# A two-layer graph kernel: narrow gathers straight into their place, the rank-9 term as nine rows of a list, three joints overlapped

## The chip, the cores and the metric

The kernel runs on one core of a Trainium2 chip. The metric is the device time of one execution in microseconds (us). Engines: PE (TensorE, matrix products), PEld (its weight loads), DVE (VectorE), ACT (ScalarE), POOL (GpSimd), SP (SyncE, which here only issues DMAs). DMAs are issued by SP, by ACT and, where the rows to be fetched stand in a list of indices, by POOL ("gathers", `DMA_INDIRECT` in the profile).

## The reference, cut to what matters

`x` is 8 x 2048 x 128 (batch, node, feature), `adj` is a 2048 x 2048 matrix, nearly all zeros, whose nonzero pattern is symmetric; the weights and the 640 x 128 `Theta1` are dense. All is float32.

```
sj = x @ w_j ; si = x @ w_i
res = si[:, :, None] + sj[:, None, :] + adj * w_r + g_b       # 8 x 2048 x 2048
x = layernorm(x + einsum('bij,bjd->bid', res, x) @ weight + bias0)
# twice the same support: A1 = A2 = adj
h1 = einsum('bnf,nw->bwf', x, adj) ; h2 = 2 * einsum('bnf,nw->bwf', h1, adj) - x
x = layernorm(x + relu(concat(x, h1, h2, h1, h2) @ Theta1 + bias))
```

The first layer splits into `adj * w_r` times Y0 = x @ weight, and a term of rank 9: the eight columns si (one for each batch) times column sums of Y0, and one row that is the same for all nodes. The second layer is done by Horner's rule: u = X1 th0, y = adj^T u + X1 th1, out = adj^T y + X1 th2, where X1 is the result of layer 0. So the matrix is applied three times: in layer 0, in "hop 1" (from u to y) and in "hop 2" (from y to out).

## The kernel before, in words

Nodes are cut into 16 chunks of 128. A row of Y0, u or y (8 batches x 128 features) is 4 KB, and a chunk of rows fills one of the slots of 128 x 1024 numbers in the tiles `Y` (16 slots), `ring` (6), `trp` (1, `spare`) and `st` (4).

Stage A (up to some 150 us): the 16 row blocks of adj are loaded (`pump`, lines 216 to 232), transposed on PE and scaled by w_r on ACT (`row_groups`). The transposed blocks go into DRAM tensors `rr_d`, beside a plain copy of the matching columns of adj. x is loaded, transposed and multiplied by the weight (`x_t`, `y_of`), and Y0 goes to DRAM (`y0_d`). Masks of nonzero 32-wide tiles are made on DVE.

Lists (120 to 193 us): DVE sorts the nonzero rows of each chunk's columns into seven lists of up to 128 row numbers: four "T" lists (each serves 32 columns of the chunk), two "H" lists (64 columns each) and a third H list (all 128 columns). A chunk of a product is then: the diagonal block (`own_rows`, line 765), four T products and three H products (`listed`, line 722), each with 128 gathered 4-KB rows as moving operand and gathered pieces of adj as weights. T lists hold only rows of chunks 0 to 13, so they can be fetched before the last two chunks are written.

The weights are gathered as well, by jobs (lines 524 to 581). For chunks 4 to 15, `get_job` gathers rows of 1 KB from `rr_d` into one of four staging slots of `st`, three or four gathers to a job, and `keep_job` masks them on DVE into `rct` (for layer 0) and `rc` (for the hops); 24 jobs, 84 gathers. Chunks 0 to 3 need pieces of adj for the hops alone: eight more jobs, 28 gathers of 512-byte rows into `trp[:, 2]`, masked by DVE into `rc`. The source text puts them last: they are kept in hop 1 (line 924).

Chunks 0 to 3 of layer 0 are multiplied in full (`full_rows`, 16 blocks each). Chunks 4 to 15 go by lists in a loop (lines 839 to 862): own rows, rank-9 term (`si_t`, a transpose of si, and `rank9`, two products with 5 rows), T, H, sum with x (`z_add`), layernorm, then `make_u` for the chunk two steps before (transposes to `x1t`, product with th0, store into `u_d`). x for the sum is loaded by `load_z` into one of four slots, and the own rows of Y0 by `own0`: chunks 4 to 7 still stand in `Y`, chunks 8 to 15 are read back from DRAM.

Gathered rows of Y0, u and y go round twelve slots of `Y` (`G`, line 710), whose slots come free when the product that reads them is done. Hops (`hop`, line 865): own rows, theta product, T and H of each chunk, begun one ahead. At the start of hop 1, two chunks are begun with their T lists while the last chunk's u is on its way.

All engines' instructions are recorded in order of the text, and a scheduler then places them; an instruction of POOL that is ready may go ahead of one that the text has earlier. The order on each queue is fixed when the program is built.

Of the kernel before, what the change touches and what calls it, by code (L numbers as in the profile page):

```python
# [18 lines left out]
def kernel(  # L19
# [36 lines left out]
    PAD = 40000  # L56
    W = 3 * P
# [57 lines left out]
    def load_constants():  # L115
        with nc.allow_non_contiguous_dma(reason="two columns of 128 numbers"):
            act.dma_start(out=wx[:, D:D + 2], in_=g_w[0:2 * D].rearrange("(t p) -> p t", p=P))
        act.dma_start(out=wx[:, 0:D], in_=weight)
        act.dma_start(out=wr, in_=g_w[2 * D:2 * D + 1][None, :].to_broadcast([P, 1]))
        act.dma_start(out=gb, in_=g_b[None, :].to_broadcast([P, 1]))  # L120
        for i in range(4):
            act.dma_start(out=b0row[:, i, :], in_=bias0[None, :])
        act.dma_start(out=b1bc[:, 0, :], in_=bias1[None, :].to_broadcast([P, D]))
        act.dma_start(out=th, in_=theta.rearrange("(m p) f -> p m f", p=P))

    ctx.enter_context(nc.allow_non_contiguous_dma(reason="512-byte rows of a block of 128 columns"))
    load_constants()
# [4 lines left out]
    e5 = const.tile([1, 5], F32)  # L132
    dve.memset(e5, 0.0)
    dve.memset(e5[:, 4:5], 1.0)
# [4 lines left out]
    sel5 = const.tile([P, 4, 5], F32)  # L139
    dve.memset(sel5, 0.0)  # L140
    for i in range(4):
        dve.tensor_copy(sel5[:, i, i:i + 1], sel[:, 0:1])
        dve.tensor_copy(sel5[:, i, 4:5], sel[:, 1 + i:2 + i])
# [3 lines left out]
    dve.tensor_copy(num, numi)  # L147
    coli = const.tile([P, NI], I32)
    pool.iota(coli[:, 0:NT], pattern=[[1, NC], [0, QT]], base=0, channel_multiplier=0)
    pool.iota(coli[:, NT:NT + 2 * NC], pattern=[[1, NC], [0, 2]], base=0, channel_multiplier=0)  # L150
# [12 lines left out]
    si = const.tile([P, NC, 37], F32)  # L163
    dve.memset(si, 0.0)
    for h in range(2):
        dve.memset(si[:, :, 32 * h + 4:32 * h + 5], 1.0)
# [34 lines left out]
    todo += [("x", 8), ("s", 12), ("x", 9), ("s", 13), ("x", 10), ("x", 11), ("s", 14), ("x", 12)]  # L201
# [11 lines left out]
    def load_z(c):  # L213
        zs[c] = load_x(c, [ring[:, 3], ring[:, 4], ring[:, 5], spare][(c - 2) % 4])

    def pump():
        while todo:
            what, n = todo[0]
            if what == "a" and n < done["a"] + 3:
                sp.dma_start(out=am[n % 3], in_=adj[R_ORDER[n] * P:(R_ORDER[n] + 1) * P, :])  # L220
            elif what == "x" and n < done["x"] + 6:
                c = X_ORDER[n]
                xin[c] = load_x(c, ring[:, X_SLOT[n % 6]])
                if c < ND:
                    zs[c] = xin[c]
            elif what == "s" and done["a"] == NC:
                store_rt(n)
            elif what == "c" and done["a"] == NC:
                copies([n])
            else:  # L230
                return
# [53 lines left out]
    def s_rows(c0):  # L285
# [5 lines left out]
        for h in range(2):  # L291
            act.copy(si[:, c4, 32 * h:32 * h + 4], sraw[:, c4, h * HB:(h + 1) * HB, 1])
# [15 lines left out]
    LAST = list(range(ND)) + list(range(8, NC)) + list(range(4, 8))  # L308
# [18 lines left out]
    pump()  # L327
    for k, n in enumerate(R_ORDER):
# [139 lines left out]
    def lists_end(part):  # L468
# [17 lines left out]
        s = slice(lo, hi)  # L486
        rown = small.tile([P, NT], F32, name=f"rown{part}", tag="rown")[:, 0:hi - lo]
# [4 lines left out]
        dve.scalar_tensor_tensor(rown, rown, float(NC), col[:, s], op0=ALU.mult, op1=ALU.add)  # L492
# [14 lines left out]
    adj128 = adj.rearrange("n (c f) -> (n c) f", f=P)  # L507
# [17 lines left out]
    for c in range(ND):  # L525
        jobs += [("T", c), ("H", c)]
    got, kept = [0], [0]
    last = trp[:, 2].rearrange("p i f -> p (i f)")

    def staged(k):  # L530
        return st[:, k % 4 * BD:] if jobs[k][1] >= ND else last

    def get_job():
# [3 lines left out]
        for n, i in enumerate(columns(c, what)):  # L537
            if c >= ND:
                gather(
                    s[:, n * 2 * P:(n + 1) * 2 * P], rr_d[c - ND].rearrange("n m f -> n (m f)"), idx,  # L540
                    i, N,
                )
            else:
                gather(s[:, n * P:(n + 1) * P], adj128, idr, i, N * NC)

    def keep_job():
# [3 lines left out]
        m = 2 if c >= ND else 1  # L550
        hc = has[:, columns(c, what)[0]:columns(c, what)[0] + QT]
        for k in range(m):
            if m == 1 or k == 1:
                to = rc[:, c * W:(c + 1) * W]
            else:
                to = rct[:, (c - ND) * W:(c - ND + 1) * W]
            of = s[:, k * P:]
            if what == "T":
                if m == 2:
                    dve.tensor_mul(  # L560
                        to[:, 0:P].rearrange("p (t f) -> p t f", t=QT),
                        strided(of, QT, m * P + TW, TW), hc[:, :, None].to_broadcast([P, QT, TW]),
                    )
                    continue
                for t in range(QT):
                    at = t * (P + TW)
                    dve.tensor_scalar(
                        to[:, TW * t:TW * t + TW], of[:, at:at + TW], hc[:, t:t + 1], None,
                        op0=ALU.mult,
                    )  # L570
                continue
            step = m * P + 64
            dve.tensor_mul(
                to[:, P:2 * P].rearrange("p (t f) -> p t f", t=2), strided(of, 2, step, 64),
                hc[:, 0:2, None].to_broadcast([P, 2, 64]),
            )
            i = NT + 2 * NC + c
            dve.tensor_scalar(
                to[:, 2 * P:3 * P], of[:, 2 * m * P:2 * m * P + P], has[:, i:i + 1], None,
                op0=ALU.mult,  # L580
            )

    def make_ub():
# [4 lines left out]
        for h in range(2):  # L588
            pe.matmul(
                pu[32 * h:32 * h + 5], e5, b0row.rearrange("p i f -> p (i f)"), start=True,  # L590
# [444 lines left out]
```

## Time and profile before

| what | value |
|---|---|
| time, median of 3 runs (lowest, highest) | 855.64 us (852.42, 857.48) |
| the profiled execution's own time | 818.08 us |
| its span, first to last instruction | 816.3 us |
| PE busy, POOL busy, DVE busy | 732.8, 445.2, 394.7 us |
| mean granted PE clock | 0.971 |
| moved by DMA | 253.90 MB, mean 311 GB/s |
| share of the 16 DMA engines' time: POOL's queue, SP's, ACT's | 49.7%, 31.1%, 8.9% |

The profiled execution is 4.4% faster than the median of the timed ones. Stages by the trace: adj and x up to 151 us, lists and full rows up to 262 us, layer 0 by lists up to 429 us, joint and hop 1 up to 625 us, hop 2 up to 801 us, and a tail up to 816 us.

How to read it: the page cuts the span into 40 slices of 20.4 us and gives the busy tenths of each engine in each; "DMA" is the mean busy share of the 16 DMA engines. A group row names engine, operation, output and input, count, busy time and mean length of one, and what the engine waited for before it. A POOL gather is busy for the time that POOL takes to issue it; the data land later. All lines of this kernel are recorded by one helper (L72), so that operations are told apart by the tiles they touch.

### The profile page before, as it was taken

The page shows a single profiled execution, that of the slowest core. Times are in us where ns is not written, and L with a number is a line of the kernel's source. Part 1 is how long each engine was busy: PE and PEld are TensorE (multiplying, and loading weights), DVE is VectorE, ACT ScalarE, POOL GpSimd, SP SyncE. Part 2 cuts the span into 40 slices and gives each one's busy share as a digit, 9 for nine tenths or more (in the row PEclk, how much of TensorE's full clock was granted, in tenths as well). Part 3 has the DMA queues.
Part 4 walks back from the last instruction along what each step waited for, and adds up shares of the span by engine and source line. Part 5 has one row for each costly group of instructions (what it writes and reads, how often), then busy time and mean ns, then how long its engine had stood idle before and what let it go on. Part 6 is the DMA issues. An engine that isn't in the chain of part 4 may idle for free.

```text
span 816.3 us, 10067 instructions
## 1 busy us (share of the span) xinstructions
PE 732.8 (90%) x3554; PEld 364.9 (45%) x3554; DVE 394.7 (48%) x591; ACT 192.7 (24%) x439; POOL 445.2 (55%) x432
## 2 busy tenths in 40 slices
PE   4999999997999998988798888898899999999992
PEld 4666566642644343434345243333344454444441
DVE  4664876578341655555533000000100377777775
ACT  3757554321200332313222000000000011111101
POOL 1000000477747876776344677776774777776740
PEclk9999999997999999999899899999999999999997
DMA  8999999999326799999969799899999799999982
GB/s 264 296 314 316 352 292 295 314 398 347 119 89 223 244 346 368 341 344 367 356 224 344 246 364 360 314 365 346 339 372 357 252 343 357 370 385 389 363 299 68
DMA packets 165299, 253.90 MB, mean 311 GB/s; under 512 B 17255, under 2 KB 118020, under 8 KB 163192
## 3 DMA queue, kind: packets, MB, share of 16 engines
q0 software_dynamic: 49280, 146.52, 49.7%
q1 hardware_dynamic: 93200, 81.01, 31.1%
q10 hardware_dynamic: 22760, 25.63, 8.9%
q8 instruction: 30, 0.49, 0.2%
q14 instruction: 29, 0.24, 0.1%
HBM read 234.82 MB, written 58.72 MB: 360 GB/s over the span
## 4 chain that ended last, share of the span: by engine, by line
PE 52%; DMA 29%; issue 6%; ACT 6%; DVE 3%; POOL 2%; ACTq 0%; POOLq 0%; SPq 0%; DVEq 0%
PE bank L72 52%; DMA Y<-u_d,idx 12%; DMA Y<-y_d,idx 8%; DMA st<-rr_d,idx 2%; DMA rd<-rr_d 2%; ACT Y L72 2%; DMA ring<-in_x_dram 2%; POOL Y L72 1%; ACT rct L72 1%; ACT trp L72 1%; DMA trp<-in_adj_dram,idr 1%; DVE s L72 1%; DVE ring L72 1%; ACT at L72 1%; DVE st L72 1%
## 5 line engine op out<-in xcount | busy, mean ns | idle before, releaser
L72 POOL DMA_INDIRECT Y<-y_d,idx x196 | 212.0, 1081 | 93.2 <-PE bank L72 38.0
L72 PE MATMUL bank<-Y,rc 128*32 128x512 f32 (+2 forms) x896 | 219.7, 618 | 21.3 <-DMA Y<-u_d,idx 19.1
L72 POOL DMA_INDIRECT st<-rr_d,idx x84 | 90.3, 1075 | 183.5 <-DVE rown L72 148.3
L72 POOL DMA_INDIRECT Y<-u_d,idx x112 | 111.8, 999 | 53.9 <-issue 29.9
L72 PEld LDWEIGHTS bank<-Y,rc 128*32 128x32 f32 (+2 forms) x896 | 58.6, 130 | 179.3 <-issue 99.5
L72 PE MATMUL bank<-Y,at 128*128 128x512 f32 x256 | 115.2, 601 | 0.0
L72 PE MATMUL bank<-Y,rct 128*32 128x512 f32 (+2 forms) x336 | 77.3, 625 | 8.5 <-DMA Y<-y_d,idx 8.5
L72 DVE TENSOR_REDUCE s<-sq 128x4 f32<-128x512 f32 x64 | 43.9, 686 | 58.0 <-ACT sq L72 58.0
L72 PEld LDWEIGHTS bank<-Y,at 128*128 128x128 f32 x256 | 47.8, 193 | 53.6 <-issue 53.4
L72 DVE COPY ring<-bank 128x512 f32<-128x512 f32 x10 | 6.9, 692 | 110.1 <-PE bank L72 110.1
L72 ACT ACTIVATE sq<-ring 128x512 f32<-128x512 f32 x44 | 27.7, 630 | 129.5 <-DVE ring L72 109.7
L72 PE MATMUL bank<-ring,rd 128*128 128x512 f32 x108 | 51.5, 599 | 5.7 <-DMA rd<-rr_d 4.1
L72 PE MATMUL bank<-ident,rc 128*128 128x128 f32 (+2 forms) x302 | 45.0, 297 | 12.6 <-DMA rc<-in_adj_dram 6.6
L72 PE MATMUL bank<-th,at 128*128 128x128 f32 x384 | 49.2, 283 | 1.9 <-ACT at L72 1.9
L72 PEld LDWEIGHTS bank<-th,at 128*128 128x128 f32 x384 | 46.8, 197 | 6.7 <-ACT at L72 3.8
L72 DVE TENSOR_TENSOR ring<-bank,ring 128x512 f32<-128x512 f32 x26 | 17.3, 688 | 66.0 <-PE bank L72 60.8
L72 DVE TENSOR_REDUCE st<-rc 128x64 f32<-128x2048 f32 x16 | 36.5, 2283 | 25.7 <-DMA rc<-in_adj_dram 25.7
L72 ACT COPY ring<-bank 128x512 f32<-128x512 f32 x34 | 19.9, 586 | 122.5 <-PE bank L72 112.9
L72 PEld LDWEIGHTS bank<-Y,rct 128*32 128x32 f32 (+2 forms) x336 | 20.8, 130 | 57.3 <-issue 32.4
L72 PEld LDWEIGHTS bank<-ident,rc 128*128 128x128 f32 (+2 forms) x302 | 33.8, 150 | 25.5 <-issue 9.1
L72 PE MATMUL bank<-wx,trp 128*128 128x130 f32 x256 | 36.9, 288 | 4.3 <-ACT trp L72 2.2
L72 PE MATMUL bank<-ident,ring 128*128 128x128 f32 x232 | 32.5, 282 | 6.4 <-DMA ring<-in_x_dram 2.8
(142 smaller groups left out, 789.1 us busy)
## 6 DMA issues: line engine op xcount, KB each, us to landing
rc<-in_adj_dram SPq DMA_DIRECT2D x16, 1024.0 KB, 10.9
ring<-in_x_dram SPq DMA_DIRECT2D x25, 512.0 KB, 8.5
rr_d<-in_adj_dram SPq DMA_DIRECT2D x12, 1024.0 KB, 10.8
rr_d<-Y SPq DMA_DIRECT2D x8, 1024.0 KB, 9.0
y_d<-Y SPq DMA_DIRECT2D x16, 512.0 KB, 10.6
u_d<-ring ACTq DMA_DIRECT2D x12, 512.0 KB, 7.0
ring<-y_d SPq DMA_DIRECT2D x11, 512.0 KB, 23.2
ring<-u_d SPq DMA_DIRECT2D x10, 512.0 KB, 3.9
```

The costliest lines, as they stand in the source:

```text
L72: return lambda *a, **k: tc.keep_in_program_order(f(*a, **k))
```

## The change

Seven things change together.

1. Start: each load of adj is cut into two halves; w_r is the first constant to be loaded, on ACT's queue, and the constants of later stages go to SP's queue, after the first eight chunks of x.
2. Pieces of adj for chunks 0 to 3: no staging and no mask by DVE. `rc[0:1536]` is zeroed by POOL, and 28 gathers write rows of 32, 64 or 128 numbers (128, 256 or 512 bytes) straight into their places; an index out of bounds leaves the zeros.
3. Jobs of the other chunks: the same 84 gathers, more of them placed before the loop of layer 0 and fewer in it.
4. Rank 9, chunks 4 to 15: the third H list is held to 119 entries, and its last nine rows carry si (in the weights, by `si_rows`) and the rows of `ub` (in two slots `C0`, by `ub_rows`). `rank9` and `si_t` stay for chunks 0 to 3 only. In this input the third lists have 73 to 112 entries.
5. x of chunks 4 to 15 is loaded into `x1t[c]`, where the transposed result is written later. Own rows of Y0 stay in place for chunks 4 to 11.
6. Slots: layer 0 gathers into ten slots (`G0`: eight of `Y`, two of `ring`) and two for the third list (`C0`); the hops use twelve of `Y` (`G1`).
7. Joints: two blocks of `full_rows(2)` go ahead of the end of the lists; hop 1 begins three chunks, not two; the last two chunks of hop 2 are done by halves of the batch (`by_halves`).

As built, POOL's queue has 58 gathers before its first gather of Y0 for a chunk's T list in the kernel before (54 of jobs, 4 of chunk 0), and 92 and the memset in the changed one (60 of jobs, all 28 direct ones, and 4 of Y0 for the third lists of chunks 4 and 5 and two T lists of chunk 5 that go ahead). The seventh and last gather for chunk 4 is the 101st, that for chunk 15 the 196th. In hop 1 no gather of adj is left (20 before).

```diff
+    LC = 96
+    R9 = 23
...
     def load_constants():
+        act.dma_start(out=wr, in_=g_w[2 * D:2 * D + 1][None, :].to_broadcast([P, 1]))
...
             if what == "a" and n < done["a"] + 3:
-                sp.dma_start(out=am[n % 3], in_=adj[R_ORDER[n] * P:(R_ORDER[n] + 1) * P, :])
+                for w in (slice(0, N // 2), slice(N // 2, N)):
+                    sp.dma_start(
+                        out=am[n % 3][:, w], in_=adj[R_ORDER[n] * P:(R_ORDER[n] + 1) * P, w]
+                    )
...
     acc0, acc1 = acc_pair(), acc_pair()
     pump()
+    load_constants()
...
     def load_z(c):
-        zs[c] = load_x(c, [ring[:, 3], ring[:, 4], ring[:, 5], spare][(c - 2) % 4])
+        zs[c] = load_x(c, x1t[c])
...
-    LAST = list(range(ND)) + list(range(8, NC)) + list(range(4, 8))
+    LAST = list(range(ND)) + list(range(12, NC)) + list(range(4, 12))
...
+        if part:
+            dve.tensor_scalar(pl[:, 2 * NC:], pl[:, 2 * NC:], free, None, op0=ALU.mult)
...
     jobs = [("T", c) for c in T_ORDER] + [("H", c) for c in range(ND, NC)]
-    for c in range(ND):
-        jobs += [("T", c), ("H", c)]
...
+    def get_direct(n):
+        for at, w, i in direct[:n]:
+            gather(
+                rc[:, at:at + w], adj.rearrange("n (c f) -> (n c) f", f=w), idr, i, N * (N // w)
+            )
+        del direct[:n]
...
+    def si_rows(c0):
+        b = by4(bank[turns[turn[0] % len(turns)]])[LC:]
+        turn[0] += 1
+        for i in range(4):
+            pe.matmul(
+                b[:, i, :], si[:, c0 + i, :], ident, start=True, stop=True, skip_group_check=True,
+                tile_position=(0, LC),
+            )
+        r = rct.rearrange("p (c w) -> p c w", w=W)
+        act.copy(r[LC:, c0 - ND:c0 - ND + 4, 2 * P:3 * P], b)
...
-    NG = 12
-    G = [flat(Y[:, n]) for n in LAST[:NG]]
+    G0 = [flat(Y[:, n]) for n in LAST[:8]] + [flat(ring[:, n]) for n in range(2)]
+    C0 = [flat(ring[:, 5]), flat(spare)]
+    G1 = [flat(Y[:, n]) for n in list(range(4)) + list(range(8, NC))]
...
     def own0(c):
-        load_own(0, y0_d, c, Y[:, c] if c < 8 else ring[:, c % 2], c < 8)
+        load_own(0, y0_d, c, Y[:, c] if c < 12 else ring[:, 3 + c % 2], c < 12)
...
     rank9(1, acc1)
+    ub_rows(C0)
+    for c in range(ND, NC, 4):
+        si_rows(c)
     rounds2([5, 6])
     next_job()
     rounds2([7])
+    acc2 = bank[4:6]
+    full_rows(2, acc2, LAST[:2])
     lists_end(1)
     z_add(acc0, zs[0])
     z_add(acc1, zs[1])
+    pool.memset(rc[:, 0:ND * W], 0.0)
...
     rank9(2, acc2)
+    next_job()
+    next_job()
     z_add(acc2, zs[2])
...
-        if c < 15:
+        if kept[0] < len(jobs):
             keep_job()
-        if c < 13 or c == 14:
+        if c % 2 == 0 and got[0] < len(jobs):
             get_job()
+        get_direct(1 if c < 10 else 2 if c < 12 else 3)
         accs = acc_pair()
         own_rows(0, c, accs, True)
         if c + 2 < NC:
             own0(c + 2)
-        rank9(c, accs)
-        if c + 1 < NC:
-            si_t(c + 1)
         listed(0, c, accs, "T")
         listed(0, c, accs, "H")
...
         begin(0)
+        if i == 1:
+            fetch(2)
+            rows(2, "T")
         between()
         begin(1)
+        if i == 1:
+            begin(2, bank[4:6])
...
         for k, c in enumerate(order):
+            if i == 2 and k >= NC - 2:
+                rows(k, "H")
+                rows(k + 1 if k + 1 < NC else NC, "T")
+                by_halves(k)
+                continue
```

In `by_halves`, for each half of the batch, PE does the transposes of X1 first, then the theta, own, T and H products of that half, and DVE and ACT work on a half (add, relu, mean, square, then scale and store 256 KB) while PE does the next.

## The prediction

> **What bounds the kernel now.** I read the page's slices first, then the busy time by stretch, then POOL's and PE's instructions in order of time.
>
> Slices of the page: PE, POOL, DMA.
>
> ```profile
> PE   4999999997999998988798888898899999999992
> POOL 1000000477747876776344677776774777776740
> DMA  8999999999326799999969799899999799999982
> ```
>
> PE, POOL and DMA are all near full from slice 15 to slice 38, so no total names the bound; slices 11 to 13 (204 to 265 us) are the only long hole of the DMA engines. Stretches of the span (us, busy time and count of PE, PEld, DVE, ACT, POOL, then PE clock, DMA share, GB/s): layer 0 by lists, joint, hop 1 with and without gathers of adj, hop 2, tail.
>
> ```profile
> 240.00:430.00 190.00, 172.01 (x792) 76.81 (x791) 95.59 (x168) 48.26 (x99) 126.23 (x122) 0.98 0.89 309
> 430.00:476.00 46.00, 37.74 (x188) 17.75 (x187) 7.41 (x12) 7.46 (x14) 26.95 (x27) 0.93 0.87 303
> 476.00:580.00 104.00, 95.03 (x430) 38.49 (x428) 8.82 (x25) 5.01 (x9) 76.38 (x78) 0.97 0.96 351
> 580.00:625.00 45.00, 42.04 (x197) 18.02 (x197) 3.26 (x6) 2.84 (x5) 32.69 (x34) 0.96 0.98 365
> 640.00:801.00 161.00, 160.95 (x821) 77.28 (x818) 121.00 (x166) 23.41 (x45) 112.80 (x99) 1.00 0.96 344
> 801.00:816.00 15.00, 0.35 (x4) 0.11 (x2) 7.40 (x10) 1.56 (x3) 0.00 (x0) 0.67 0.25 74
> ```
>
> Hop 2 is bound by PE (160.95 of 161), the tail by a DVE chain. For the rest, POOL in order of time:
>
> ```profile
> 223.66 1.00 POOL L72 DMA_INDIRECT st<-rr_d,idx  x1 [0.30 <-issue]
> 224.96 0.99 POOL L72 DMA_INDIRECT st<-rr_d,idx  x1 [0.30 <-issue]
> 234.74 1.00 POOL L72 DMA_INDIRECT st<-rr_d,idx  x1 [8.79 <-DVE rc L72]
> ...
> 239.55 1.00 POOL L72 DMA_INDIRECT Y<-y_d,idx  x1 [0.31 <-issue]
> ...
> 554.83 1.00 POOL L72 DMA_INDIRECT trp<-in_adj_dram,idr  x1 [0.30 <-issue]
> ```
>
> A gather costs POOL 1.0 us and 0.3 us until the next, 1.30 us whatever its width: 128 KB for `st` or 440 KB for `Y`. From 476 to 580 us it issues 78 in 104 us, hardly pausing: its queue, not the products, sets hop 1. PE's theta products, one row where a chunk begins, show it:
>
> ```profile
> 571.78 1.95 PE L72 MATMUL bank<-th,at 128*128 128x128 f32 x16
> 581.88 1.95 PE L72 MATMUL bank<-th,at 128*128 128x128 f32 x16
> 596.49 1.95 PE L72 MATMUL bank<-th,at 128*128 128x128 f32 x16
> 605.63 1.95 PE L72 MATMUL bank<-th,rct 128*128 128x128 f32 x16
> 614.77 1.95 PE L72 MATMUL bank<-th,rct 128*128 128x128 f32 x16
> ```
>
> A chunk after gathers of adj takes 14.6 us (581.88 to 596.49), without them 9.14 us, which is PE's own work.
>
> **What the Trainium skill says.** "DMA: Bandwidth & Descriptors", Issuing engines are not separate DMA queues: all issuers share 16 DMA engines. The trace agrees: the queues' shares add to 89.7% of the span, so bytes from any queue compete. The same page, Specifications: below 512 B a transfer loses line rate; the page counts 17,255 packets under 512 B but not whose, so no run here shows what the change's 128-byte rows cost. "TensorE: Matmul & The Clock Gate", its table of properties: GpSimd's queue is strict FIFO; the 8.79 us wait above held 2 more adj gathers and then the first Y0 gather, which agrees. The same page, Part 1: The HAM clock gate: an idle window of about 3.4 us halves PE's clock; after a wait of 4.58 us at 451.66 us the H products of two chunks took 11.68 us, 5.84 each, against 3.85 for a chunk's at full clock, which agrees.
>
> **Step 1, start: -3 us.** PE first has x at 16.48 us, after idling 1.22, 0.68 and 2.79 us; SP waited 4.9 us for a constant's DMA before it could issue x at 6.54. Halves let PE begin earlier, and x no longer waits for that constant. From then on PE and ACT take turns at 12.4 us per two blocks without a DMA wait. Gain between 0 (DMA share is 1.02 from 20 to 151 us, so earlier demand may find no data) and 4.7 us (the three idles); I take 3. The moved constants (0.4 MB, about 1.2 us of DMA) lie where x is prefetched.
>
> **Step 2, POOL ahead of chunk 4: +19 us.** The first job is issued at 151.7, now 148.7. 92 gathers x 1.30 us, the memset (1.4 us, as `st`'s 128x1536 took) and about 1 us of waits for `st` slots put the first T gather of chunk 4 at 271, against 239.55. Its last is number 101: 148.7 + 2.4 + 100 x 1.30 = 281; landing 6.5 us (median of `st` gathers; `Y` 8.4 in a full queue), last products 2 us: chunk 4 ends at 290. Before, it ended at 270.8. The 8.79 us wait goes, as two jobs are kept ahead of `z_add(acc2)`. An added wait: DVE now keeps five H jobs (chunks 4 to 8) ahead of chunk 3's sum, the last gathered near 280 and landed near 286; behind it stand chunk 3's sum and layernorm and chunk 4's sum, and PE, which needs chunk 3's banks for chunk 5. That falls near 290, so it is hidden; uncovered it would cost the few us by which 286 passes the need. x for chunk 4 and on waits for what was in `x1t` (loads of `Y` rows, pieces of `rct`); behind it on SP's queue stand diagonal blocks and own rows, a chunk ahead of their use. PE, done with full rows at 262, will idle some 20 us and cool; this costs nothing while gathers are late. 128-byte rows: no gain below their bytes, and at most the packet time of the 512-byte rows they replace (3,584 packets either way), so within 1 us of DMA, in the hole.
>
> **Step 3, layer 0 by lists: -3 us at its end.** Three limits from chunk 8, whose last gather is number 144, at 337, and which ends at 346. POOL: number 196 at 405, end 413. PE: a chunk takes 11.81 us now (298.81 to 310.62); minus rank 9 (1.06) and si's transpose (0.23), 10.5: 346 + 7 x 10.5 = 419.5. DMA: seven Y0 gathers 8.5 us (440 KB at the POOL queue's 361 GB/s: 146.52 MB in 49.7% of the span), u store 1.5, diagonal 0.2, and for 7 chunks 3 loads of x and 4 of Y0 at 1.64 (SP's queue: 319 GB/s): 11.8 a chunk, 429, less half a chunk to a whole one fetched ahead (6 to 12): 417 to 423, and above it the waits of a queue that must hold three issuers in step. I take 426, against 429.3. It spares 4 Y0 loads (6.6 us of DMA) and 15.5 us of PE. The 96+32-row masks add a 0.3 us DVE instruction per chunk, and `si_rows`, `ub_rows` 5 us of PE and 5 us of ACT before 200 us, where PE idled 3.46 and 1.87.
>
> **Step 4, joint: -8 us.** Before, the third chunk's last product ended 47 us after layer 0 (476.4). u of chunk 15 is stored at +18; then 9 H gathers (11.7 us), landing 6.5, product 2: +38.3, where 47 were; I take -8. Before, 3.29 us of waiting for DVE, three adj gathers (3.9 us) and two T gathers (2.6 us) stood among these. The begun third chunk fills PE's 4.58 us wait. `rows(2, "T")` stands ahead of the H gathers, but has its slots and u by then. The T gathers that take slots 0 and 1 of `Y` now wait for chunk 15's H products; queued behind them on POOL are the other T gathers and the nine H gathers, and `begin(0)` waits for them, with chunk 15's transposes behind it on PE. They land near +7.5, when `begin(0)` is due, so I add nothing; late, each us counts once.
>
> **Step 5, hop 1's pace: -14 us.** 13 chunks took 148.8 us (476.4 to 625.2), 11.45 each. POOL: 7 x 1.30 = 9.1. PE: 9.14. DMA: 8.5 + 0.2 + y store 1.5 + own u 1.2 = 11.4 by the same prices, which overstate: the trace had 11.0 a chunk (0.96 of 11.45) with gathers of adj in it. I take 10.4, between 9.14 and 11.2.
>
> **Step 6, hop 2: 0; tail: -3.5 us.** PE's 11.6 us a chunk don't change. The tail was
>
> ```profile
> 801.39 0.69 DVE L72 SCALAR_TENSOR_TENSOR st<-st,bank 128x512 f32<-128x512 f32 x1 [0.46 <-PE bank L72]
> ...
> 810.87 0.38 ACTq L72 DMA_DIRECT2D out_dram<-st  x1
> ```
>
> and 5.4 us of store. By halves, DVE's chain after the last product is 2.9 us (two sums 1.4, mean 0.8, subtraction 0.65), then two ends of 2.4 us, 7.7; the store is half the bytes, 4.3; PE's 1.04 us of transposes moves ahead. 15.9 becomes 12.0 to 13.
>
> **Sum:** -3 (step 1 is in step 3's end), -8, -14, -3.5: -28.5 on 818.08, 789.6, a ratio of 0.965. 818.08 is the span of 816.3 and 1.8 us around it, which stay. The timed runs' median is 1.046 times the profiled time; I apply the ratio to that median: 826 us.
>
> **Rivals.** (a) *DMA holds the pace, and the late start is never made up.* Place: layer 0 after chunk 4. For it: the DMA share of 0.89 from 240 to 430 us. Chunks 5 to 15 took (429.3 - 270.8) / 11 = 14.4 us each; if they keep that, layer 0 ends at 290 + 11 x 14.4 = 448 (+19); joint -8, pace of hop 1 unchanged (0.96), tail -3.5: +7.5, 825.6, so 863. Against it: chunks before carried three adj gathers, ten issues of 1.30 us, near their whole pace. It decides from a layer-0 end of 441 (13.7 us a chunk), if hop 1 gains nothing. (b) *PE is the next bound.* Layer 0 ends at 420 (-9), joint -9, hop 1 at 9.6 us a chunk (-24), tail -4.5: -46.5, 771.5, so 807. For it: chunks at 605 and 614 us. (c) *Hidden anyway:* layer 0 ends 12 later, joint -8, hop 1 at 11.2 (-3), tail -3.5: -2.5, so 853. That the work isn't spread as said is part of (a): as built, the direct gathers aren't spread over loop and hop but stand in one block.
>
> **Chances.** Forecast 0.54, (b) 0.19, (c) 0.12, (a) 0.15. A measurement here can tell 0.5%, 4 us. Half of (c) lies within it, a third is faster. So faster 0.77, same 0.07, slower 0.16. Range 803 to 857: a little beyond the values of (b) and (c), so that most of both lies in it; the bounds of steps 3 (-9 to +12) and 5 (-24 to -3) make it, and (a) is left out.
>
> **What would show it.** First T gather of chunk 4 near 271 and a PE hole of some 20 us ahead of chunk 4; chunks at 9 to 12 us from chunk 8; third chunk of hop 1 at +38; no `trp` gathers and 10.4 us a chunk in hop 1; the tail near 12. Wrong if layer 0 ends after 441, or hop 1 keeps 11.4 with POOL pausing.

## The result, and the profile after

The changed kernel took 868.49 us (855.75 to 876.58, 22 runs), the kernel before 855.56 us (847.11 to 867.41, 22 runs) on the same chip: a ratio of 1.0119, 95% interval 1.008 to 1.0158. It is 1.2% slower. The prediction had 826 us, 803 to 857, and faster.

The chips used here differ. The kernel before took 810 to 812 us on two of them (the quick chips below) and 850 to 856 on the others; ratios are taken within a chip. On the slower chips the runs of one kernel spread over 2% to 4%, and a ratio is taken over the runs within 1.5% of each kernel's quickest, so it can differ from that of the medians.

The changed kernel's profiled execution took 869.73 us, its span is 867.5. Its slices of 21.7 us, PE, POOL and DMA:

```profile
PE   5988999679830869879999889999999889999993
POOL 1000001556777574766662556665665567777640
DMA  8999999992233455898997989999999689999982
```

PE has a hole in slices 12 and 13 (239 to 282 us), and the DMA engines are at two to five tenths from slice 10 to 16. Before, PE had no slice under 7 between the first and the last. Part of the hole stands out in PE's instructions (start, length, instruction, and in brackets the idle time ahead of it and what ended it):

```profile
247.24 0.39 PE L74 MATMUL bank<-ident,si 128*5 128x128 f32 x4
285.34 2.35 PE L74 MATMUL bank<-ub,sit 5*128 5x512 f32 x4 [37.71 <-ACT sit L74]
```

and in ACT's:

```profile
257.58 0.33 ACTq L74 DMA_DIRECT2D u_d<-ring  x1
285.03 0.53 ACT L74 COPY sit<-bank 5x128 f32<-5x128 f32 x2 [27.48 <-remote]
```

The four small products ended at 247.63, but ACT copied their result only at 285.03, 37.4 us later, though it had nothing to do from 257.9 on. On the quick chips, up to the tail, no product is reported more than 0.9 us after it ended. So I read the steps of the prediction on such a chip, with the same changed kernel (run e11 below: span 824.7, against the profile of before with 816.3, whose chip is not on record but whose time fits the quick ones). Its slices:

```profile
PE   5999899999996358999988799999999899999993
POOL 1000000677777777775545376656663777776640
DMA  9999999995444668999988999999998899999971
```

The hole is there too, but shorter: slices 13 to 15 (247 to 309 us). POOL, 7 tenths busy all through it, is at its issue rate (1.0 of 1.30 us). POOL's instructions around the end of the block:

```profile
273.56 1.00 POOL L74 DMA_INDIRECT Y<-y_d,idx  x1 [0.30 <-issue]
...
302.88 1.00 POOL L74 DMA_INDIRECT st<-rr_d,idx  x1 [0.31 <-issue]
304.19 1.67 POOL L74 DMA_INDIRECT Y<-y_d,idx  x1 [0.30 <-issue]
```

Ahead of these, all 28 direct gathers stand between 192 and 269 us, in runs of 6, 2, 10, 8 and 2 among the gathers of the jobs; "block" below means this. 273.56 is the first T gather of chunk 4 (239.55 before). 304.19 is an H gather of chunk 5; it stands behind six gathers of the jobs. PE waits for both:

```profile
277.89 1.88 PE L74 MATMUL bank<-Y,rct 128*32 128x512 f32 x2 [11.15 <-DMA Y<-y_d,idx]
...
308.96 1.97 PE L74 MATMUL bank<-Y,rct 128*64 128x512 f32 x2 [6.56 <-DMA Y<-y_d,idx]
```

Later stretches, as in the prediction (busy time and count of PE, PEld, DVE, ACT, POOL, PE clock, DMA share, GB/s): end of layer 0, hop 1.

```profile
340.00:430.00 90.00, 84.14 (x414) 40.21 (x413) 55.09 (x88) 27.73 (x51) 56.62 (x55) 1.00 1.00 365
478.00:580.00 102.00, 96.40 (x431) 41.09 (x430) 7.62 (x11) 6.45 (x11) 64.18 (x65) 0.98 0.98 362
```

POOL is no longer the bound in these stages, as forecast; the DMA engines are full, and PE nearly so. In milestones, by the end of the last product of a chunk's third H list (us):

| stage | before | after (e11) | difference | predicted |
|---|---|---|---|---|
| chunk 4 of layer 0 done | 270.9 | 292.1 | +21.2 | +19 |
| chunks 5 to 15 | 158.6 | 150.2 | -8.4 | -22 |
| layer 0 done | 429.5 | 442.3 | +12.8 | -3 |
| joint, to hop 1's third chunk | 47.1 | 47.5 | +0.4 | -8 |
| 13 chunks of hop 1 | 148.7 | 141.5 | -7.2 | -14 |
| 14 chunks of hop 2 | 154.1 | 153.7 | -0.4 | 0 |
| last two chunks of hop 2 | 21.1 | 26.6 | +5.5 | 0 |
| after the last product | 15.8 | 13.1 | -2.7 | -3.5 |
| span | 816.3 | 824.7 | +8.4 | -28.5 |

The profile of before (818.08 us) is some 8 us longer than the 810.39 us median of that kernel beside e11, so the table shows the loss that much too small; in which of its rows the rest would fall is not known.

### The profile page after: what moved, and what is told of

Same layout as the page of the kernel before. It is cut to its first block, busy times and chain, and to the rows that moved or that the text cites. A ratio compares the mean times of both kernels' runs of the same rounds, so it can differ in the third digit from the quotient of the medians.

```text
span 867.5 us, 10065 instructions
## 1 busy us (share of the span) xinstructions
PE 734.0 (85%) x3534; PEld 369.1 (43%) x3534; DVE 396.4 (46%) x603; ACT 195.0 (22%) x440; POOL 444.1 (51%) x433
## 3 DMA queue, kind: packets, MB, share of 16 engines
q0 software_dynamic: 49280, 145.59, 47.1%
## 4 chain that ended last, share of the span: by engine, by line
PE 53%; DMA 22%; issue 9%; ACT 6%; another core or an unknown queue 6%; POOL 2%; DVE 1%; POOLq 0%; ACTq 0%
PE bank L74 53%; DMA Y<-u_d,idx 11%; DMA Y<-y_d,idx 5%; ACT Y L74 2%; POOL Y L74 2%; DMA ring<-y_d,idx 2%; ACT trp L74 1%; ACT rct L74 1%; DMA trp<-y_d,idx 1%; DMA y_d<-st 1%; DMA ring<-in_x_dram 1%; DVE st L74 1%; DMA wr<-in_L_gnn_g_w_dram 1%; ACT at L74 1%
## 5 line engine op out<-in xcount | busy, mean ns | idle before, releaser
L74 POOL DMA_INDIRECT Y<-y_d,idx x170 | 185.0, 1088 | 105.4 <-PE bank L74 51.4
L74 POOL DMA_INDIRECT st<-rr_d,idx x84 | 85.8, 1021 | 189.6 <-DVE rown L74 144.4
L74 PE MATMUL bank<-th,at 128*128 128x128 f32 x384 | 52.3, 291 | 14.3 <-issue 14.1
L74 ACT COPY ring<-bank 128x512 f32<-128x512 f32 (+1 forms) x36 | 20.8, 585 | 156.2 <-PE bank L74 90.0
L74 PE MATMUL bank<-ub,sit 5*128 5x512 f32 x16 | 8.4, 1053 | 49.0 <-ACT sit L74 40.6
L74 PE MATMUL bank<-Y,rct 128*32 128x512 f32 (+1 forms) x232 | 45.8, 607 | 0.7 <-DMA Y<-y_d,idx 0.6
L74 PEld LDWEIGHTS bank<-ident,rc 128*128 128x128 f32 (+2 forms) x302 | 34.9, 155 | 25.2 <-issue 9.5
L74 PE MATMUL bank<-ring,rd 128*128 128x512 f32 x92 | 43.5, 594 | 1.2 <-issue 1.2
L74 ACT ACTIVATE sq<-ring 128x512 f32<-128x512 f32 x26 | 16.4, 630 | 121.1 <-DVE ring L74 96.5
L74 PEld LDWEIGHTS bank<-wx,trp 128*128 128x128 f32 x256 | 31.9, 194 | 16.0 <-ACT sraw L74 8.4
L74 ACT COPY trp<-bank 128x512 f32<-128x512 f32 (+1 forms) x38 | 21.2, 586 | 62.0 <-PE bank L74 59.6
```

What stands on the lines that cost most here:

```text
L74: return lambda *a, **k: tc.keep_in_program_order(f(*a, **k))
```

## The experiments

**Theory.** The 28 direct gathers, as a block ahead of chunk 4's in POOL's queue, delay layer 0, and nothing after it has the slack to win that back. **Rivals.** The loss comes from the changed order of the front, slots and own rows; from the narrow rows as such; or the gathers cost their issue time wherever they stand.

**1. The direct gathers alone (e3, e12), beside the changed kernel (e4, e11) and the kernel before (e1).** To the kernel before is added part 2 alone, where the changed kernel has it:

```diff
+    pool.memset(rc[:, 0:ND * W], 0.0)
...
+        get_direct(1 if c < 10 else 2 if c < 12 else 3)
```

and the jobs of chunks 0 to 3 are taken out.

> The kernel before, unchanged, profiled a second time: its page is of an execution of 818 us, and the 22 timed ones lie at 847 to 867. Theory A (the late start of layer 0 is made by POOL's longer queue alone): this execution shows no waits that end with no work recorded, as the first did, PE is done with full rows near 262 us and chunk 4 near 271, and the span is near 816 or spread evenly longer by some other cause. Theory B (PE reports finished products late in some stretch of most executions, whatever the kernel, and the page of before was of an execution without it): this one has a span near 850, PE idle for 20 to 40 us between 150 and 290 us with the releaser not named, and chunk 4 ends at 295 to 310.

> The kernel before with part 2 of the change alone: no adj jobs for chunks 0 to 3, a memset and 28 direct gathers in their place, which stand in one block ahead of the first gather of Y0 for chunk 4. Theory A (POOL's queue ahead of chunk 4): layer 0 starts 24 x 1.3 = 31 us later (four adj gathers stood there before), hop 1 gains 14 us at most: 10 to 20 us slower than before, ratio 1.01 to 1.025, with chunk 4 ending near 302. Theory B (late reports of PE): not told by the queue; ratio 1.03 or more if narrow gathers are what brings the late reports, 1.00 if they have nothing to do with it.

> The changed kernel, unchanged, profiled a second time. In its first profile PE's products for chunk 1's u and the full rows of chunk 3 were reported up to 37 us after PE's last record (waits of 37.7 and 8.4 us near 250 and 320 us). Theory B1 (late reports come with the front of this kernel): again 30 to 45 us of such waits between 230 and 330 us, u of chunk 2 stored near 340, span near 865. Theory B2 (they fall at random): they lie elsewhere or sum to under 15 us in that stretch, u of chunk 2 stored before 320, span 840 to 850.

> The changed kernel, unchanged, on a chip beside the kernel before. In the last call the kernel before ran at 812 us with no late products of PE, in the two calls ahead of it, on another chip, at 850 to 853 with them. Theory A (POOL's longer queue in front makes the loss, late products only add to it): where the kernel before runs at 812, chunk 2's u is stored 30 to 35 us later than in the page of before (near 306), the loop and the joint win back some 15, hop 1 some 5, the tail costs 3: ratio 1.005 to 1.02. Theory G (the loss is made by late products alone): there the changed kernel has none, and the ratio is 0.97 to 0.985 as predicted. Where the kernel before runs at 850, a ratio of 1.005 to 1.02 tells nothing new.

> The kernel before with part 2 alone in one block, as once before, beside the changed kernel on the same chip. Theory A: where the kernel before runs at 812, chunk 2's u is stored 24 x 1.3 = 31 us or less later than there (near 300), 15 us come back in the loop (fewer gathers), 5 in the joint, 5 in hop 1: ratio 1.00 to 1.012. Theory G: 0.985 or less, as nothing is late.

On a quick chip e12 took 826.9 us, a ratio of 1.0214 (1.0164 to 1.0263), and e11 827.26, 1.0218 (1.0169 to 1.0266): part 2 alone costs as much as the whole change, so the other six parts together win nothing net there. POOL's queue in e12:

```profile
264.04 1.00 POOL L72 DMA_INDIRECT Y<-y_d,idx  x1 [0.30 <-issue]
```

Chunk 4's first T gather is 24.5 us late, chunk 4 is done 19.6 us late (290.5), layer 0 18.6 (448.1); joint and hop 1 then regain 9.0. Between 255 and 440 us PE waits 21.4 us for rows of Y0 in e12 and 28.2 in e11, where it waited 8.5 before. On a slower chip e3 had 1.0143 (1.0053 to 1.0233). There e1 took 845.26 us (849.99 the median of before) and e4 859.55 (852.65), one run each.

**2. The gathers left out (e8, e14, e18).** Both kernels without the gathers of adj for chunks 0 to 3, the lines above deleted but for the memset (in e8 the jobs of these chunks too). So a part of both hops' result is left out; the products themselves are still issued.

> The kernel before without any gather of adj for chunks 0 to 3: their pieces in rc are zeroed by POOL before chunk 2 and stay zero, so the hops leave out those four chunks' listed products' content (the products themselves are still issued). It gives the floor for every placing of these gathers. Theory D (short gathers bring stretches in which PE reports products late, wherever they stand): no waits over 5 us for late products in hop 1, u of chunk 2 near 296, the loop 155 to 160, joint 32, hop 1 140: span near 822, ratio 0.955 to 0.975. Theory E (late reports come anyway): hop 1 keeps stretches of late products, ratio 0.98 or more.

> The changed kernel with its 28 direct gathers left out, the memset kept: the pieces of adj for chunks 0 to 3 in the hops stay zero, so a part of both hops' result is left out. Theory (POOL's queue ahead of chunk 4 sets the loss): u of chunk 2 is stored about 24 us earlier than in the changed kernel, the loop gives a part of that back, and the whole is 18 to 30 us shorter, a ratio of about 0.98 to 0.99 to the kernel before. Rival (the loss lies in the other parts, the front order, the slots, the own rows): it is at most 8 us shorter than the changed kernel and stays over 1.00.

> The changed kernel with its 28 direct gathers left out (a part of both hops' result with them), beside it. Theory: the floor of every placement of these gathers, a ratio of 0.98 to 0.99, and the first gather of Y0 for chunk 4 some 10 us ahead of the changed kernel's 273.6. Rival: the put-together version is level with it, within 0.3%, if its gathers are hidden.

e8, the kernel before without them: 801.16 us against 811.51, 0.988 (0.9848 to 0.9912). This is the most that any placement of the gathers could bring there: 10 us. Its hop 1:

```profile
460.00:600.00 140.00, 133.15 (x622) 56.98 (x622) 8.99 (x13) 7.62 (x13) 89.31 (x91) 1.00 0.98 366
```

No gather of adj is left, and POOL is no bound (91 gathers of 1.30 us in 140 us), yet a chunk takes 11.0 us (143.1 for 13). The DMA engines are at 0.98, so I read them as the bound; no run took load off them.

e14, the changed kernel without them: 836.54 us against 850.37, 0.9847 (0.9756 to 0.9937); e18 on another chip 0.9829 (0.9742 to 0.9916). Beside e14 the changed kernel itself (e13) had 859.01 us, 1.0131 (1.0102 to 1.0161).

> The changed kernel, nothing edited, as the measure for the three runs beside it. Both theories expect a ratio of 1.010 to 1.023 to the kernel before, as in the two earlier comparisons.

So the gathers cost the changed kernel 2.8% of 850, some 24 us (1.0131 - 0.9847; by the intervals give or take 8). Chunk 4 is done at 303.4 us in e14 and at 333.3 in e13. That settles the first rival on these chips: order, slots and own rows don't make the loss. On a quick chip the changed kernel without the gathers was not run.

**3. Other places (e2, e5, e6, e9, e10).** e2: in the changed kernel, the gathers after layer 0, four to a chunk of hop 1.

```diff
-    pool.memset(rc[:, 0:ND * W], 0.0)
...
-        get_direct(1 if c < 10 else 2 if c < 12 else 3)
...
-                get_direct(1)
+                get_direct(4)
...
+    pool.memset(rc[:, 0:ND * W], 0.0)
```

The last line stands ahead of hop 1's loop in the program's order.

> The changed kernel, but the memset and the 28 direct gathers of adj for chunks 0 to 3 are put between layer 0 and hop 1, four to a chunk in hop 1; all else as changed. Theory A (POOL's queue): 28 x 1.30 + 1.4 = 38 us go from the queue ahead of chunk 4, so chunk 4 ends 30 to 40 us earlier than in the changed kernel (338 us there), hop 1 gets back up to 13 us as POOL has 10 gathers a chunk for some chunks; total 835 to 850, ratio to before 0.975 to 0.99. Theory B (late reports of PE, independent of the direct gathers): PE still stalls some 40 us near 250 us, chunk 4 ends at 325 or later, ratio 1.00 to 1.02.

1.0309 (1.0238 to 1.038). As built, six of them stand between layer 0's gathers and hop 1's (439 to 447 us), two single ones follow, and twenty come in fours within hop 1 (497 to 566 us). Joint and hop 1 are 43.2 and 153.7 us by their stores, 32.5 and 141.1 in the changed kernel's first profile, 23.3 more together; u of chunk 15 is stored at 472.9 us, not 497.8, 24.9 earlier. A miss: the cost moved, and the ratio is no better than 1.0119.

e5 (to the kernel before) and e6 (to the changed one) spread them, seven to each of four chunks of the loop, with a memset that holds them there:

```diff
+        if c in (9, 11, 13, 15):
+            d = (c - 9) // 2
+            pool.memset(rc[:, d * W:(d + 1) * W], 0.0)
+            get_direct(7)
```

> The kernel before with part 2 alone, as in the last run, but really spread: rc is zeroed in four pieces of 128x384 by POOL in chunks 9, 11, 13 and 15 of the loop of layer 0, and the seven direct gathers of a chunk can only follow its piece. Theory A (the queue ahead of chunk 4 costs, hop 1 without gathers of adj gains): u of chunk 2 is stored near 296 as in the second profile of before (325 with the gathers in one block), the loop grows by 0 to 10 us, joint and hop 1 keep the 10 and 14 us that the block had gained: ratio 0.970 to 0.985. If the gain in hop 1 is only the time moved to the front, ratio 0.995 or more.

> The changed kernel with its direct gathers spread in the same way over chunks 9, 11, 13 and 15, all else as changed. Theory A: u of chunk 2 near 311 as with the gathers in hop 1, joint 32 and hop 1 141 us as in the changed kernel: 20 to 30 us faster than the changed kernel, ratio to before 0.985 to 1.0. If the other parts of the change are what makes its front late, it stays some 15 us behind the kernel before with spread gathers.

1.0147 (1.0096 to 1.0197) and 1.0255 (1.02 to 1.031): no better than in a block. e9 (to the kernel before) and e10 (to the changed one) spread them singly over chunks 8 to 15, each with its own memset; e10 also has the order of front and full rows of the kernel before:

```diff
+            pool.memset(rc[:, at:at + w], 0.0)
             gather(
...
+            if c > 7:
+                get_direct(2)
...
+            if c > 7:
+                get_direct(1 if c < 12 else 2)
```

> The kernel before with part 2 alone, the direct gathers put one at a time: each piece is zeroed by POOL and gathered, two or one between the T and H gathers and after the H gathers of chunks 8 to 15, so that no two direct gathers stand together. Theory D1 (a series of short gathers slows PE, single ones do not): the late products of 10 to 15 us in chunks 11 to 15 that the seven-at-a-time spread showed are gone, loop 160 to 170 (203 there), ratio 0.97 to 0.985. Theory D2 (each short gather costs PE time, however it is placed): the loop stays at 190 to 205, ratio 1.005 to 1.02.

> The changed kernel with two things put back: the order of the front (jobs, full rows of chunks 2 and 3 and their sums) as in the kernel before, and the direct gathers one at a time in chunks 8 to 15. Left of the change are the start by halves, rank 9 as rows, x in x1t, own rows in place, the slots, the joint and the tail. Theory F (the front's order makes the changed kernel late even without the block): u of chunk 2 near 292 to 300 where 311 and 324 were seen with the changed order, and with D1 a ratio of 0.965 to 0.985, at or below the kernel before with the same gathers. If rank 9 as rows or x in x1t make the front late, u of chunk 2 stays at 310 or later.

e9: 1.0096 (1.0069 to 1.0123); e10: 1.0065 (1.0045 to 1.0086). Both start chunk 4 on time (done at 271.3 and 268.7 us), both lose in the loop. Waits between 300 and 425 us (total, times, longest), without the gathers (e8):

```profile
PE bank L72 <- DMA Y<-y_d,idx: 6.6, 7, 1.2
...
POOL Y L72 <- PE bank L72: 32.9, 27, 15.8
```

and with them (e9):

```profile
PE bank L72 <- DMA Y<-y_d,idx: 16.5, 12, 2.5
...
POOL Y L72 <- PE bank L72: 4.2, 11, 1.5
```

POOL has 32.9 us of waits for slots in this stretch, and 28 gathers of 1.30 us are 36.4, their memsets apart. They use up the slack (4.2 left), and beyond that PE waits for rows. On the chip of e8 and e9, where the kernel took 801.16 us without any gather of adj, the places of the kernel before cost 10.4 us and those of e9 18.0; the block costs some 27 (those 10 and the 16.5 of e12, on the other quick chip). So the third rival is right in part: in no place that was tried are the gathers free, but the place decides how much of their time is lost.

**4. Narrow rows (e7).** e3 with its 28 gathers of 1-KB rows into scratch instead; the pieces of adj for chunks 0 to 3 are left out of the hops.

```diff
+            k = (28 - len(direct)) % 6
             gather(
-                rc[:, at:at + w], adj.rearrange("n (c f) -> (n c) f", f=w), idr, i, N * (N // w)
+                rc[:, k * 2 * P:(k + 1) * 2 * P], rr_d[0].rearrange("n m f -> n (m f)"), idx, i, N
             )
```

> The kernel before with 28 more gathers in one block ahead of chunk 4, as with the direct gathers, but each fetches 1-KB rows of a DRAM tensor into a scratch part of rc, not rows of 128 to 512 bytes; the pieces of adj for chunks 0 to 3 are left out of both hops (what stands there is multiplied in their place). Theory A (the number of gathers counts): as with the narrow ones, u of chunk 2 near 325, ratio 1.005 to 1.025. Theory C (rows of 128 bytes slow PE down): PE has no stretch of products 2.1 or 2.8 us apart between 240 and 300 us, u of chunk 2 at 300 to 310, ratio 0.985 to 1.0.

1.0115 (1.0045 to 1.0185), and e3 1.0143 (1.0053 to 1.0233): the intervals overlap. So the block costs time with wide rows too, and no cost of the narrow ones is shown, though one of about 1% would not be seen here.

**5. The halves (e15).** The changed kernel with the last two chunks of hop 2 done whole.

```diff
-            if i == 2 and k >= NC - 2:
+            if i == 3:
```

> The changed kernel without the halves of part 7: the last two chunks of hop 2 go as the others do. Theory (the halves cost more of TensorE's time than they spare behind it): the time from the out store of chunk 13 to the end falls from 29.7 to 26 or 27 us, 3 us in all, 0.996 to 0.997 of the changed kernel. Rival (the prediction's step 6): the tail is 3.5 us longer without them.

1.0024 (0.9985 to 1.0063) to before, the changed kernel 1.0131 beside it; the medians, 858.61 and 859.01, don't differ, so the total leaves it open. The stage doesn't: from the store of chunk 13 to the end (PE, PEld, DVE, ACT, POOL, clock, DMA share, GB/s), with halves (e13),

```profile
833.50:863.30 29.80, 16.07 (x77) 6.01 (x75) 17.35 (x32) 3.38 (x8) 2.16 (x2) 0.85 0.32 104
```

and without (e15),

```profile
827.20:853.20 26.00, 11.45 (x65) 6.20 (x63) 15.88 (x22) 3.12 (x6) 0.00 (x0) 0.82 0.34 112
```

All profiles of kernels with halves have 29.4 to 30.1 us here, all without 25.9 to 27.0. PE and POOL with halves (e13):

```profile
828.65 1.07 PE L74 MATMUL bank<-Y,rc 128*64 128x512 f32 x2 [0.43 <-DMA Y<-y_d,idx]
...
843.74 1.13 PE L74 MATMUL bank<-Y,rc 128*128 128x512 f32 x2 [0.40 <-DMA Y<-y_d,idx]
...
836.12 1.18 POOL L74 DMA_INDIRECT Y<-y_d,idx  x1 [6.44 <-PE bank L74]
```

The two second halves take PE 5.4 us each (832.52 to 837.93, 844.70 to 850.11), the two first halves 7.9 and 7.1 (824.77 to 832.69, 837.77 to 844.87). A first half reads all seven lists in about half of a chunk's time, so PE comes to the H lists before their rows are there. For chunk 15 a wait of POOL adds to this: its last two gathers wait 6.44 us for slots, since a slot comes free only when the second half of the chunk ahead has read it.

**6. A version put together (e16, e17).** Front order as in the kernel before, no halves, three direct gathers in each of chunks 12 to 15, the other 16 two to a chunk in hop 1.

```diff
+            if c > 11:
+                get_direct(2)
...
+            if c > 11:
+                get_direct(1)
...
-        get_direct(1 if c < 10 else 2 if c < 12 else 3)
...
-            if i == 1:
-                get_direct(1)
+            if i == 1 and k < 8:
+                get_direct(2)
```

> A version put together from the runs: the changed kernel with the order of front and full rows of the kernel before, 3 direct gathers in each of chunks 12 to 15 of layer 0 and 2 in each of the first eight chunks of hop 1, and no halves in hop 2. Theory: u of chunk 2 at the time of the kernel before or earlier (272 where that has 275), loop 162 to 170 us, hop 1 11.0 a chunk, tail 26: a ratio of 0.985 to 0.995. Rival (the 28 gathers cost their 36 us wherever they stand, since POOL's and the DMA engines' time is short in both stages): 1.00 or above.

> The put-together version once more, on a chip drawn anew, as its medians left the sign open. Theory: where TensorE's products report on time, loop 162 to 175 us, hop 1 at most 144, tail 26: a ratio of 0.985 to 0.997. Rival (the gathers cost their 36 us wherever they stand): 1.00 or above.

e16: 0.992 (0.9885 to 0.9954), with medians of 853.49 and 850.37 that say the opposite; e17 on another chip: 1.0028 (0.9991 to 1.0064), medians both 856.34. No gain over the kernel before is shown. It has none of what e18, beside e17, has without the gathers (0.9829). Both ran on slower chips; on a quick one it has not run.

## Why the prediction was wrong, point by point

**Step 1 (-3) and step 2 (+19): right.** The first job was issued at 147.3 us (predicted 148.7), the first T gather of chunk 4 at 273.56 (271), gather 101 at 284.0 (281), and chunk 4 was done at 292.1 (290). The prediction saw the block and priced it rightly; what failed is what it set against it.

**Step 3 (-3 at layer 0's end): this failed, by 15.8 us.** The +19 was to be won back in chunks 5 to 15. Two terms fell. Gather 144, the last of chunk 8, came at 342.3, not 337 (gather 101 was 3 us late, and three of the issues after it took 1.6 to 1.8 us), and chunk 8 was done at 353.6, not 346. Then seven chunks took 88.7 us, 12.7 each, where 426 - 346 gives 11.4: six at 12.4 with a DMA share of 0.94 to 1.02, the last at 14.6 with 0.62. My own DMA sum was 11.8 a chunk; I took "half a chunk to a whole one fetched ahead" off. Nothing was fetched ahead by then, since POOL issued every gather of chunks 4 to 8 without a pause and PE waited for them. And landing took longer in a full queue than the 6.5 and 8.4 us used (POOL gathers from 340 to 430 us in e11: count and median us from issue to landing):

```profile
Y<-y_d,idx POOLq DMA_INDIRECT x34, 11.3
```

Layer 0 ended at 442.3, beyond the 441 from which rival (a) was to decide. The place of rival (a) was right, with 0.15; its pace of 14.4 us a chunk was too slow (13.7 from chunk 5 to 15). That its total, 825.6 us, is close to e11's is luck in part: it had the joint 8 us shorter and hop 1 unchanged.

**Step 4 (-8): it lost 0.4.** The H gathers wait for u of chunk 15 to land. Their first, before and in e11:

```profile
447.43 0.99 POOL L72 DMA_INDIRECT Y<-u_d,idx  x1 [6.85 <-DMA u_d<-st]
466.24 0.98 POOL L74 DMA_INDIRECT Y<-u_d,idx  x1 [10.40 <-DMA u_d<-st]
```

That is 17.9 us after layer 0's last product before, as the sum had it (18), and 23.9 in e11. The prediction had named the cause and set it at nothing ("so I add nothing; late, each us counts once"): PE's first T products of hop 1 wait for their rows, and chunk 15's transposes stand behind them. In e11:

```profile
453.10 1.90 PE L74 MATMUL bank<-Y,rc 128*32 128x512 f32 x10 [1.33 <-DMA Y<-u_d,idx]
454.94 1.09 PE L74 MATMUL bank<-ident,rct 128*128 128x128 f32 x8
```

The 16 T products of hop 1's first chunk take from 449.19 to 455.00, 5.8 us instead of 1.9, and the transposes begin 12.7 us after layer 0's last product instead of 8.9; from u's store to that first H gather it is then 7.3 us (5.1 before). From the ninth H gather to the third chunk's end 13.2 us pass, where the sum had 9.8. The begun third chunk fills PE's idle time but is not on this path. One reading of PE's lines was loose too: the H products of the two chunks from 451.66 on did not take 5.84 us each, but 7.9, most of it at a granted clock of 0.50, and then 3.85.

**Step 5 (-14): right in kind, half in size, -7.2.** 10.9 us a chunk, not 10.4. e8, with no adj gather at all, has 11.0. The prediction worked out 11.4 from DMA prices, called it overstated, and took a value between PE's pace and 11.2; the 11.0 us of DMA time that it had read from the trace would have been nearer. The lines that it gave for PE's pace of 9.14 us held the answer: the two chunks of 9.14 come right after one of 14.6, and the three together take 32.9 us, 11.0 each.

**Step 6 (-3.5): wrong in sign, +2.8.** After the last product 2.7 us are won (3.5 predicted). The step had set the change in the products of the last two chunks at nothing; they take 26.6 us instead of 21.1. What was left out is the rows: a first half needs all seven lists early, and halves keep the slots longer, so that POOL's last gathers wait (experiment 5).

**The sum.** 15.8 + 8.4 + 6.8 + 5.5 + 0.8 - 0.4 = 36.9 us of misses, which is 28.5 + 8.4. And e8 says that the kernel before gains 10 us when its gathers of adj for chunks 0 to 3 go altogether, so most of the 28 was never to be had by moving them: with POOL's load lighter, a chunk of hop 1 still took 11.0 us, where it had taken 11.45.

**The scale.** The page's ratio was applied to the timed median as if the 4.6% between them were spread evenly. It isn't: against the profile of before, e1 on a slower chip has chunk 4 done 15.2 us later and 11.7 us more in hop 1; against e11, the first profile of the changed kernel has chunk 4 done 46.3 us later. The changed kernel's longest wait of PE in layer 0 on the slower chips was 37.7, 39.3 and 34.9 us in three profiles, 11.1 and 11.6 without the direct gathers (e14, e18), 3.0 in the kernel before (e1). The predicted 826 us is by chance the time on a quick chip, where the kernel before takes 810.

## What to carry to other kernels

A queue that issues in order has to be drawn up against the first moment at which its consumer needs it: work that may be done at any time still costs its whole issue time if it stands ahead of the gathers on the path. Before a move, measure the slack of the place it goes to, here POOL's waits for slots (32.9 us for 36.4 us of gathers), and take the nearest full resource as the new pace, not a mean with the next. When an end is cut into halves, ask when the first half needs its inputs, and which buffers are then held longer.

## What the runs showed of the hardware that I had not expected

In the profiles of the slower chips PE's results reach their consumers late, or its products come slowly, in stretches of layer 0. In e3, whose products of this form take 0.44 us each up to 260 us (35 in 15.25), they then come so:

```profile
279.68 1.01 PE L72 MATMUL bank<-Y,at 128*128 128x512 f32 x1 [1.79 <-issue]
282.47 1.01 PE L72 MATMUL bank<-Y,at 128*128 128x512 f32 x1 [1.79 <-issue]
```

2.8 us from one to the next, with no wait on record. Narrow rows are not needed for it: in e7, with 1-KB rows, PE waits 24.31 us ahead of 274.13. Nor are the direct gathers, as e14 has waits of 11.1 us without them.

What causes it stays open. Instructions are not lost from these profiles (10,065 in the changed kernel's first profile as in e11), but semaphore updates, the signals by which finished work releases what waits for it, are: the packed traces of the 14 profiles on slower chips hold 6,308 to 7,392 of them, those of e8 to e12 and of before 11,461 to 12,187, and they are missing for every engine (DVE's: 337 against 500 in these two profiles of the changed kernel). So what such a profile names as the end of a wait is unsure, and a rival stands untested: that the recording itself, and not the chip, holds the engines up there.

Most gathers' issues cost POOL 1.00 us and 0.30 to the next, whether their rows have 128 bytes or 4 KB; in e11 379 of 420 took less than 1.1 us, the longest 2.03.
